# More third-level Strassen steps in a two-layer projection kernel, and some vector work moved to its opening

## The chip, the cores and the metric

The kernel runs on one core of a Trainium2 chip. The metric is the device time of one execution in microseconds; less is better. Everything is fp32.

## The reference, cut to what matters

`x` is 8 x 256 tokens by 1024. Two layers, each with its residual:

```python
# layer 0: one shared weight W, and a rank-16 update per expert, two of eight experts per token
base  = einsum('btd,od->bto', x, W)
gates = softmax of the top 2 of (x @ Wr.T + 5 * one_hot(language_ids)), spread over 8 experts
h     = einsum('btd,erd->bter', x, A)
x     = x + base + 2.0 * einsum('bter,bte,eor->bto', h, gates, B)
# layer 1: every batch row b has its own weight, chosen by an id
x     = x + einsum('bsi,boi->bso', x, weight[adapter_ids])
```

## The kernel before, in words

**The product x W.** It is done by the Strassen-Winograd scheme: with both matrices cut into two by two blocks, seven block products take the place of eight, at the price of sums of blocks. The scheme is used twice. On the first level x, W and the result are cut into halves of 512 (`xb`, `wb`, `yb`, with keys "11" to "22"), and the seven products are called by their keys "1" to "7"; the program does them in the order 1, 2, 5, 6, 3, 7, 4. Product 1 is `opening`, the others are calls of `product`. On the second level, every product is again seven: P1, P2, and so on, on quarters. These pass through three pairs of PSUM banks, called A, X and B. P1 is computed in A, copied to X by ScalarE, and both go on as accumulators; B takes P5 and P3. From one product to the next the roles of the three pairs rotate (`role[:] = [x, b, a]`), so that the next product's A is the pair that was X, and its B the pair that was A.

**The third step.** A second-level product is four matmuls of 512 columns, or, where its number stands in the `leaves` of `make_subs`, seven matmuls of 256 columns: the "leaf" of `third`. Its sums r1 to r4 (128 elements a row) and q1 to q4 (256) are made by VectorE, and its own partial results, P1 and P5, need a bank each, from which `take` evicts them into the result in four parts (of P1, P6, P5 and P7). For leaf 3 these banks are the two of pair X, for the others the two single banks (`singles`), which also serve the gate logits and the transposes of the gates (`turn(1, singles("ps_g_1"))`, after product 2). Before, leaf 2 is taken in all six products after the opening, leaf 3 in product 5, and leaf 4 in products 5, 3 and 4; the opening has leaves 3 and 4 of its own.

**The order of the vector work.** It is set while the program is built, under a manual schedule. `queue` holds vector work that can be done early: the sums of the following products, the first-level sums S1 to S4 of W (`w_sum`), the gates of the second half. A planner keeps two clocks, `now["pe"]` and `now["dve"]`, adds the cost of each instruction by `us(n)`, and puts queued work into VectorE's stream where its clock is behind TensorE's (`ahead`), or at the latest where a matmul needs it (`force`). Evictions are placed by `after` when their matmul is done. VectorE then executes in this order.

**Other work.** `project` makes the gate logits and the low-rank inputs, `gating` the gates. The low-rank update is added inside the products by matmuls with `up[rows]` and `hg`; for the rows "d" they read `bdiff`, the differences of B's rows (`b_differences`). Layer 1 is `adapt`, once per batch row: seven matmul groups in A, X and B with one Strassen-Winograd step, its sums placed by `pump`. Its first unit follows product 4.

Of the kernel before, what the change touches and what calls it, by code (L numbers as in the profile page):

```python
# [25 lines left out]
def kernel(  # L26
# [43 lines left out]
    TQ = TH // 2  # L70
# [219 lines left out]
    def gating(j):  # L290

        m1, hot1, ops1 = first_max(lg[j], j, 1)
        rest = rtile([P, C, E], "rest")
        m2, hot2, ops2 = first_max(rest, j, 2)
        dm = rtile([P, C], "dm")
        ex = rtile([P, C], "ex")
        den = rtile([P, C], "den")
        g1 = rtile([P, C], "g1")
        g2 = rtile([P, C], "g2")
        wide = [P, C, E]  # L300

        def onto_h():
            h = hT[j].rearrange("p c (e r) -> p (c e) r", r=R)
            g = hot1.rearrange("p c e -> p (c e)").unsqueeze(2).to_broadcast([P, C * E, R])
            tt(h, h, g, ALU.mult)


        ops = ops1 + [
            lambda: nc.vector.scalar_tensor_tensor(rest, hot1, NEG, lg[j], ALU.mult, ALU.add)
        ] + ops2 + [  # L310
            lambda: minus(dm, m2, m1),
            lambda: nc.scalar.activation(ex, dm, AF.Exp),
            lambda: nc.vector.tensor_scalar(den, ex, 1.0, None, ALU.add),
            lambda: nc.vector.reciprocal(g1, den),
            lambda: nc.vector.tensor_scalar(g1, g1, SCALING, None, ALU.mult),
            lambda: tt(g2, g1, ex, ALU.mult),
            lambda: tt(hot1, hot1, g1.unsqueeze(2).to_broadcast(wide), ALU.mult),
            lambda: tt(hot2, hot2, g2.unsqueeze(2).to_broadcast(wide), ALU.mult),
            lambda: add(hot1, hot1, hot2),
        ]  # L320
        return [(0.23, f) for f in ops] + [(1.22, onto_h)]

    def turn(j, banks):

# [22 lines left out]
    queue = []  # L347
    done = {}

    def us(n):  # L350
        return (n + 151) / 960

    def vec(t, fn, key=None):
        fn()
        now["dve"] += t
        done[key] = now["dve"]

    def event(name, later=0.0):
        events[name] = now["pe"] + later
# [52 lines left out]
    def third(key, leaf, lhs, rhs, place, what):  # L412

        ra = lambda i, j: lhs()[:, j, ts(i, P)]
        rb = lambda i, j: rhs()[:, i, ts(j, NQ)]
        n0, n1 = slice(0, NQ), slice(NQ, TQ)
        t, own = {}, {}
        at = {"r13": 0, "r2": P, "r4": 2 * P, "q13": 3 * P, "q2": 3 * P + NQ, "q4": 3 * P + 2 * NQ}  # L420
        me = f"{key}:L{leaf}"

        def op(name, tag, fn, x, y, what):
            width = P if name[0] == "r" else NQ

            def run():
                if place == 0:
                    t[name] = sub3.tile([P, width], F32, name=f"{name}_{key}{leaf}", tag=tag)
                else:
                    t[name] = spare(1536 + (place - 1) * 1152 + at[tag], width)  # L430
                fn(t[name], *(t[v] if isinstance(v, str) else v() for v in (x, y)))

            return us(width), what, f"{me}.{name}", run

        A, B = (lambda i, j: lambda: ra(i, j)), (lambda i, j: lambda: rb(i, j))
        ops = [
            op("r1", "r13", add, A(1, 0), A(1, 1), what),
            op("q1", "q13", minus, B(0, 1), B(0, 0), what),
            op("r2", "r2", minus, "r1", A(0, 0), what),
            op("q2", "q2", minus, B(1, 1), "q1", what),  # L440
            op("r4", "r4", minus, A(0, 1), "r2", what),
            op("q4", "q4", minus, B(1, 0), "q2", what),
        ]
        ops3 = [
            op("r3", "r13", minus, A(0, 0), A(1, 0), (f"{me}.5",)),
            op("q3", "q13", minus, B(1, 1), B(0, 1), (f"{me}.5",)),
        ]

        def piece(n, acc=None, banks=None):
            if n in (1, 5):  # L450
                own[n] = (single(f"P{n}_{key}{leaf}", n // 5) if banks is None else banks[n // 5])[:, n0]
            for x in {3: ("r4",), 4: ("q4",), 5: ("r1", "q1"), 6: ("r2", "q2", "P1"), 7: ("r3", "q3", "P6")}.get(n, ()):
                force(f"{me}.{x}")
            out_, l, r = {
                1: lambda: (own[1], ra(0, 0), rb(0, 0)),
                2: lambda: (acc[:, 0, n0], ra(0, 1), rb(1, 0)),
                3: lambda: (acc[:, 0, n1], t["r4"], rb(1, 1)),
                4: lambda: (acc[:, 1, n0], ra(1, 1), t["q4"]),
                5: lambda: (own[5], t["r1"], t["q1"]),
                6: lambda: (own[1], t["r2"], t["q2"]),  # L460
                7: lambda: (own[1], t["r3"], t["q3"]),
            }[n]()
            nc.tensor.matmul(out_, lhsT=l, rhs=r, start=(n in (1, 5)), stop=True, skip_group_check=True)  # L463
            now["pe"] += 0.432
            event(f"{me}.{n}", 0.2)

        def take(n, dest, base=None, sub=False):

            cut = lambda v: {1: v[:, 0, n0], 6: v[:, 0, n1], 5: v[:, :, n1]}[n]
            if n == 7:  # L470
                cut = lambda v: v[:, 1, :].rearrange("p (j n) -> p j n", j=2)
            src = own[5 if n == 5 else 1]
            if n in (5, 7):
                src = src.unsqueeze(1).to_broadcast([P, 2, NQ])
            evict(NQ if n in (1, 6) else TQ, cut(dest), src, None if base is None else cut(base), f"{me}.P{n}", sub)

        return ops, ops3, piece, take

    def make_subs(key, w, x, leaves=(), what=(), last=(), place=0):

# [32 lines left out]
        if 3 in leaves:  # L515
            deep[3] = third(key, 3, lambda: t["s2"], lambda: b(1, 1), 1, (f"{key}:P6",))
        if 4 in leaves:
            deep[4] = third(key, 4, lambda: a(1, 1), lambda: t["t2"], 2, (f"{key}:P6",))
        subs[key] = (a, b, t, late, deep)
        return [  # L520
            op("s1", add, a(1, 0), a(1, 1), what),
# [17 lines left out]
    def multiply(up=None, tokens=None):  # L539


        def mm(acc, lhs, rhs, first=False, rows=None, c=0, part=(0, 1), ms=(0, 1), need=()):
            if rows == "d":
                force("bdiff")
            for key in need:
                force(key)
            steps = [(lhs[:, k, ts(m, P)], rhs[:, k, :], m) for k in part for m in ms] if part else []
            if up is not None and rows is not None:
                steps += [(up[rows][:, ts(m, P)], hg[tokens][:, c, :], m) for m in ms]
            for i, (l, r, m) in enumerate(steps):  # L550
                nc.tensor.matmul(  # L551
                    acc[:, m, :],
                    lhsT=l,
                    rhs=r,
                    start=(first and i < len(ms)),
                    stop=(i >= len(steps) - len(ms)),
                    skip_group_check=True,
                )
                now["pe"] += 0.859

        return mm

    def opening(key, dest):
# [85 lines left out]
        chunk(7)  # L649
        piece(7)  # L650
        out(7, q2)
        out(5, q2, q2)
        add(q2, A, q2)

    def product(key, base, dest, lora=None, tokens=None, sub=False, joined=None):
# [66 lines left out]
        if 3 in deep:  # L722
# [19 lines left out]
            piece(7)  # L742
            take(7, at[1], at[1], sub)
            take(5, at[1], at[1], sub)
        else:
            mm(B, t["s2"], b(1, 1), False, "d", 1, need=K("s4", "B5"))
        put(1, B, True, "B3")
        join(1)
        if 4 in deep:
            if 3 not in deep:  # L750
                piece4(5)
                piece4(6)
                take4(6, at[2], old[2], sub)
                force(f"{key}.A7")
                mm(A, None, None, False, "1", 0, part=())
            for n in (2, 3, 4):
# [228 lines left out]

    opening("1", y21)
    done.clear()
    now["pe"], now["dve"] = 0.0, 3.5
    after(0.4, lambda: take(0, 1))
    for i, (t, f) in enumerate(gating(0)):  # L990
        vec(t, f, "gates0")
    project(1, 0, halves(pair("ps_h_1_0", 2)))
    now["pe"] += 7.5
    subs2 = make_subs("2", "12", "21", (2,))
    run(subs2[:2])
    after(0.4, lambda: take(1, 0))
    run(subs2[2:])
# [11 lines left out]
    event("T2", 30.0)  # L1009
    queue += [(t, (), f"gate{i}", f) for i, (t, f) in enumerate(gating(1))]  # L1010
    gates = queue[-1][2]
    queue += [(0.69, (), "I22", lambda: add_identity(wb["22"]))]
    queue += w_sum(minus, "21", "22", "21", (), "S1")
    queue += [(2.0, (), "bdiff", b_differences)]
    queue += make_subs("5", "21", "12", (2, 3, 4), ("T1",), "2", 1)
    product("2", y21, y11, 0, 0)
    force(gates)
# [3 lines left out]
    add_raw("21", 1, 1)  # L1021
    event("T3", 30.0)
    queue += w_sum(add, "11", "21", "11", (), "S2")
    queue += make_subs("6", "11", "22", (2,), ("T2",), "5", 0)
    product("5", None, y22, 1, 1)
    raw("12", 1, 1)
    event("x22", 14.0)
    queue += w_sum(minus, "12", "11", "12", (), "S4")
    queue += make_subs("3", "12", "12", (2, 4), ("x22",), "6", 1)
    product("6", y21, y21, sub=True)  # L1030
    add_raw("22", 1, 0)
# [3 lines left out]
    product("3", y22, y12, 2, 1, joined=(y12, y21))  # L1035
    load_w1(0, "21", "12", "22", "11")
    event("w0", 18.0)
    queue += make_subs("4", "22", "22", (2, 4), ("T4",), "7", 1)
    product("7", y21, y21, joined=(y22, y21))
    queue += [(t, ("w0",), f"w0_{i}", f) for i, (t, _, f) in enumerate(prep_w1(0, 0))]  # L1040
    y0 = []
# [2 lines left out]
        y0[:] = y0 or prep_y(0)  # L1044
        y0[i][2]()

    queue += [(0.69, ("4:P7", "7:join2"), f"y0_{i}", lambda i=i: prep_y0(i)) for i in range(4)]
    product("4", y21, y21, 1, 0)
    for q in list(queue):
        q[3]()  # L1050
# [57 lines left out]
```

## Time and profile before

| | us |
|---|---|
| median of three runs (lowest, highest) | 425.71 (425.32, 426.33) |
| the profiled execution, its own time | 425.69 |
| its span, first to last instruction | 423.7 |
| TensorE busy | 418.8 |
| VectorE busy | 287.6 |
| ScalarE busy | 40.6 |
| GpSimd busy | 17.6 |
| product 2 starts, with the transposes before it | 58.4 |
| product 5 starts | 90.6 |
| product 6 starts | 120.3 |
| the adapter units start | 227.8 |

How to read it: the profile is of one execution, in us from the first instruction. The lines of vector work all carry one number, L228, that of the helper that issues them; tiles tell them apart (y is a result block, s and t are sums of the second level, r and q of the third; many sums lie in spare room of x11 and show as x). L551 are matmuls of 512 columns, L463 those of the third step, L256 the projections, L326 the transposes of the gates, L863 the adapter units. Matmuls are pipelined: their shown durations overlap, and the step from one start to the next is what each costs in a stream.

### The profile page before, as it was taken

The page shows a single profiled execution, that of the slowest core. Times are in us where ns is not written, and L with a number is a line of the kernel's source. Part 1 is how long each engine was busy: PE and PEld are TensorE (multiplying, and loading weights), DVE is VectorE, ACT ScalarE, POOL GpSimd, SP SyncE. Part 2 cuts the span into 40 slices and gives each one's busy share as a digit, 9 for nine tenths or more (in the row PEclk, how much of TensorE's full clock was granted, in tenths as well). Part 3 has the DMA queues.
Part 4 walks back from the last instruction along what each step waited for, and adds up shares of the span by engine and source line. Part 5 has one row for each costly group of instructions (what it writes and reads, how often), then busy time and mean ns, then how long its engine had stood idle before and what let it go on. Part 6 is the DMA issues. An engine that isn't in the chain of part 4 may idle for free.

```text
span 423.7 us, 3569 instructions
## 1 busy us (share of the span) xinstructions
PE 418.8 (99%) x1294; PEld 226.1 (53%) x1294; DVE 287.6 (68%) x439; ACT 40.6 (10%) x69; POOL 17.6 (4%) x26
## 2 busy tenths in 40 slices
PE   8999999999999999999999999999999999999996
PEld 6579975445655454554555444444444444444574
DVE  1645699957888989878786666765747666665531
ACT  2010120022110000000000101010101101010110
POOL 1000020110001101103000000000000000000000
PEclk9999999999999999999999999999999999999999
DMA  8995089476220964918902384666658385650202
GB/s 274 385 397 236 2 173 210 126 184 101 100 99 4 179 215 78 294 24 155 342 0 99 116 321 159 242 214 213 224 194 300 109 298 190 213 183 0 101 0 99
DMA packets 20257, 72.61 MB, mean 171 GB/s; under 512 B 1552, under 2 KB 3856, under 8 KB 15248
## 3 DMA queue, kind: packets, MB, share of 16 engines
q1 hardware_dynamic: 15088, 58.87, 38.0%
q0 software_dynamic: 3904, 12.58, 16.6%
q10 hardware_dynamic: 1248, 0.93, 0.7%
q8 instruction: 10, 0.16, 0.1%
q14 instruction: 7, 0.06, 0.0%
HBM read 55.61 MB, written 8.39 MB: 151 GB/s over the span
## 4 chain that ended last, share of the span: by engine, by line
PE 99%; POOL 0%; ACT 0%; issue 0%; POOLq 0%
PE A L863 23%; PE A L551 21%; PE B L551 13%; PE B L863 13%; PE ps_h L256 7%; PE X L863 6%; PE P L463 5%; PE A_last L930 3%; PE X L551 3%; PE X L463 2%; PE A L463 1%; PE idle L568 1%; PE B L463 1%; PE ps_g L326 0%; ACT z L960 0%
## 5 line engine op out<-in xcount | busy, mean ns | idle before, releaser
L551 PE MATMUL A<-t,s 128*128 128x512 f32 x112 | 50.3, 592 | 0.0
L863 PE MATMUL B<-x,x 128*128 128x512 f32 x96 | 43.2, 592 | 0.0
L863 PE MATMUL A<-w,x 128*128 128x512 f32 x88 | 39.6, 592 | 0.0
L228 DVE TENSOR_TENSOR w<-w,w 128x1024 f32<-128x1024 f32 x24 | 29.1, 1223 | 15.1 <-PE A L863 15.1
L863 PE MATMUL A<-w,y 128*128 128x512 f32 x88 | 39.1, 592 | 0.0
L256 PEld LDWEIGHTS ps_h<-y,x 128*128 128x128 f32 x256 | 31.7, 190 | 3.3 <-issue 2.9
L551 PEld LDWEIGHTS A<-t,s 128*128 128x128 f32 x112 | 21.2, 190 | 21.2 <-issue 20.6
L256 PE MATMUL ps_h<-y,x 128*128 128x136 f32 x256 | 31.9, 279 | 0.0
L863 PEld LDWEIGHTS B<-x,x 128*128 128x128 f32 x96 | 18.2, 190 | 22.1 <-issue 22.0
L863 PEld LDWEIGHTS A<-w,x 128*128 128x128 f32 x88 | 16.7, 190 | 21.0 <-issue 21.0
L863 PEld LDWEIGHTS A<-w,y 128*128 128x128 f32 x88 | 16.7, 190 | 20.6 <-issue 20.6
L228 DVE TENSOR_TENSOR y<-P,y 128x512 f32<-128x512 f32 (+1 forms) x31 | 17.6, 567 | 14.0 <-PE P L463 9.1
L228 DVE TENSOR_TENSOR y<-A,y 128x1024 f32<-128x1024 f32 x17 | 20.8, 1223 | 8.3 <-issue 4.6
L551 PE MATMUL A<-x,w 128*128 128x512 f32 x56 | 25.4, 594 | 0.0
L551 PE MATMUL B<-x,s 128*128 128x512 f32 x40 | 18.0, 592 | 0.0
L228 DVE TENSOR_TENSOR x<-w,x 128x1024 f32<-128x1024 f32 (+1 forms) x11 | 10.6, 968 | 10.8 <-PE A L863 7.8
L225 ACT ACTIVATE z<-A 128x512 f32<-128x512 f32 x12 | 7.2, 597 | 101.4 <-PE A L863 101.4
L228 DVE TENSOR_TENSOR w<-x,w 128x1024 f32<-128x1024 f32 x8 | 9.7, 1225 | 10.2 <-PE A L863 5.7
L551 PEld LDWEIGHTS A<-x,w 128*128 128x128 f32 x56 | 10.3, 190 | 10.8 <-issue 10.5
L228 DVE TENSOR_TENSOR z<-z,X 128x512 f32<-128x512 f32 x7 | 4.8, 687 | 15.9 <-PE X L863 15.9
L551 PE MATMUL B<-t,s 128*128 128x512 f32 x32 | 15.0, 595 | 0.0
L863 PE MATMUL X<-w,y 128*128 128x512 f32 x32 | 14.4, 592 | 0.0
(179 smaller groups left out, 555.8 us busy)
## 6 DMA issues: line engine op xcount, KB each, us to landing
x<-w_dram SPq DMA_DIRECT2D x24, 1024.0 KB, 5.1
x<-xT_dram SPq DMA_DIRECT2D x10, 1024.0 KB, 10.6
w<-w_dram SPq DMA_DIRECT2D x8, 1024.0 KB, 4.8
out_dram<-z SPq DMA_DIRECT2D x15, 512.0 KB, 3.0
x<-x POOLq DMA_DIRECT2D x4, 1024.0 KB, 9.9
x<-xT_dram POOLq DMA_DIRECT2D x4, 1024.0 KB, 9.3
y<-y POOLq DMA_DIRECT2D x8, 512.0 KB, 5.3
w<-wT_dram SPq DMA_DIRECT2D x3, 1024.0 KB, 15.3
```

The costliest lines, as they stand in the source:

```text
L225: nc.scalar.activation(out_, x, AF.Copy, scale=scale)
L228: nc.vector.tensor_tensor(out_, x, y, op)
L256: nc.tensor.matmul(ps[v][:, u * EA : (u + 1) * EA], lhsT=xk(k, j, c)[:, ts(r, P)], rhs=aw_sb[:, k, :], start=(first and k == some[0] and u ...
L463: nc.tensor.matmul(out_, lhsT=l, rhs=r, start=(n in (1, 5)), stop=True, skip_group_check=True)
L551: nc.tensor.matmul(acc[:, m, :], lhsT=l, rhs=r, start=(first and i < len(ms)), stop=(i >= len(steps) - len(ms)), skip_group_check=True,)
L568: nc.tensor.matmul(idle[:, 0, :P], lhsT=ident, rhs=ident, start=True, stop=True)
L863: nc.tensor.matmul(accs[name], lhsT=lhs[:, k // 2, k % 2, :], rhs=rhs[:, k, :], start=(first and k == 0), stop=(k == KH - 1), skip_group_c ...
L930: nc.tensor.matmul(acc, lhsT=lhs[:, k // 2, k % 2, :], rhs=rhs[:, k, ts(v, m)], start=(first and k == 0), stop=(k == KH - 1), skip_group_c ...
```

## The change

Product 2 takes leaf 4 also (with its sums in a free part of y12), product 6 leaf 4, and product 4 leaf 3. Where leaf 4 is taken without leaf 3, its pieces 5 and 6 now stand between the two halves of B's accumulation, instead of after it. The identity on w22, the sum S1 of W and the differences of B's rows are no longer queued for product 2 but issued in the opening, ahead of the last evictions. S4 is queued before product 5 instead of after it. The planner's constants change: `us(n)` is (n + 66) / 960 instead of (n + 151) / 960, a result counts as ready 0.1 us after its instruction's cost, VectorE's clock starts at 6.0 instead of 3.5, and some listed costs follow.

```diff
@@ gating
-        return [(0.23, f) for f in ops] + [(1.22, onto_h)]
+        return [(0.26, f) for f in ops] + [(us(2 * TQ), onto_h)]
@@ the planner
     def us(n):
-        return (n + 151) / 960
+        return (n + 66) / 960
     def vec(t, fn, key=None):
         fn()
         now["dve"] += t
-        done[key] = now["dve"]
+        done[key] = now["dve"] + 0.1
@@ third
+                elif place == 3:
+                    t[name] = flat(yb["12"])[:, 2048 + at[tag] : 2048 + at[tag] + width]
@@ make_subs
-            deep[4] = third(key, 4, lambda: a(1, 1), lambda: t["t2"], 2, (f"{key}:P6",))
+            deep[4] = third(key, 4, lambda: a(1, 1), lambda: t["t2"], 3 if early else 2, (f"{key}:P6",))
@@ multiply
-            if rows == "d":
-                force("bdiff")
@@ opening
         out(7, q2)
+        add_identity(wb["22"])
+        for f in w_sum(minus, "21", "22", "21"):
+            f[3]()
+        b_differences()
         out(5, q2, q2)
         add(q2, A, q2)
@@ product
+        elif 4 in deep:
+            mm(B, t["s2"], b(1, 1), False, "d", 1, ms=(0,), need=K("s4", "B5"))
+            piece4(5)
+            mm(B, t["s2"], b(1, 1), False, "d", 1, ms=(1,))
+            piece4(6)
+            take4(6, at[2], old[2], sub)
         else:
             mm(B, t["s2"], b(1, 1), False, "d", 1, need=K("s4", "B5"))
...
         if 4 in deep:
             if 3 not in deep:
-                piece4(5)
-                piece4(6)
-                take4(6, at[2], old[2], sub)
                 force(f"{key}.A7")
@@ the order of the products
-    now["pe"], now["dve"] = 0.0, 3.5
+    now["pe"], now["dve"] = 0.0, 6.0
-    subs2 = make_subs("2", "12", "21", (2,))
+    subs2 = make_subs("2", "12", "21", (2, 4), early=True)
-    queue += [(0.69, (), "I22", lambda: add_identity(wb["22"]))]
-    queue += w_sum(minus, "21", "22", "21", (), "S1")
-    queue += [(2.0, (), "bdiff", b_differences)]
...
-    queue += make_subs("6", "11", "22", (2,), ("T2",), "5", 0)
+    queue += make_subs("6", "11", "22", (2, 4), ("T2",), "5", 0)
+    queue += w_sum(minus, "12", "11", "12", (), "S4")
     product("5", None, y22, 1, 1)
     raw("12", 1, 1)
     event("x22", 14.0)
-    queue += w_sum(minus, "12", "11", "12", (), "S4")
...
-    queue += make_subs("4", "22", "22", (2, 4), ("T4",), "7", 1)
+    queue += make_subs("4", "22", "22", (2, 3, 4), ("T4",), "7", 1)
```

More of the change, by code (lines that the diff above doesn't have):

```diff
@@ L477, in third, with make_subs @@
         return ops, ops3, piece, take
-    def make_subs(key, w, x, leaves=(), what=(), last=(), place=0):
+    def make_subs(key, w, x, leaves=(), what=(), last=(), place=0, early=False):
         before = (f"{last}:P7",) if last else ()
@@ L1045, in prep_y0 @@
         y0[i][2]()
-    queue += [(0.69, ("4:P7", "7:join2"), f"y0_{i}", lambda i=i: prep_y0(i)) for i in range(4)]
+    queue += [(0.6, ("4:P7", "7:join2"), f"y0_{i}", lambda i=i: prep_y0(i)) for i in range(4)]
     product("4", y21, y21, 1, 0)
```

## The prediction

> **What bounds the kernel now.** I read the page's busy shares, the chain that ended last, that chain in order of time, and then the timeline where one product hands over to the next.
>
> ```profile
> PE 418.8 (99%) x1294; PEld 226.1 (53%) x1294; DVE 287.6 (68%) x439; ACT 40.6 (10%) x69; POOL 17.6 (4%) x26
> ...
> PE 99%; POOL 0%; ACT 0%; issue 0%; POOLq 0%
> ```
>
> TensorE is the bound and does not pause: 99% of the chain is its own work, and the list of waits names none of TensorE after 38 us. So a matmul removed is worth its whole time, and every new wait of TensorE costs its whole length. VectorE is 68% busy, which says nothing of single moments. Two lines of the chain in order of time price the matmuls:
>
> ```profile
> 118.72 1.29 PE A L463 x6
> ...
> 137.27 3.43 PE B L551 x8
> ```
>
> A matmul of the program is two instructions. At 512 columns (L551) one takes 3.43 / 8 = 0.429 us, at 256 columns (L463) 1.29 / 6 = 0.215 us.
>
> The timeline at the end of product 5 and at the end of product 4, the last one before the adapter stage:
>
> ```profile
> 108.19 0.69 DVE L228 TENSOR_TENSOR y<-P,y 128x512 f32<-128x512 f32 x1 [1.78 <-ACT y L223]
> 108.99 1.23 DVE L228 TENSOR_TENSOR y<-X,y 128x1024 f32<-128x1024 f32 x1
> ...
> 118.76 1.42 DVE L228 TENSOR_TENSOR y<-X,y 128x512 f32<-128x512 f32 x2 [0.97 <-PE X L463]
> ...
> 120.28 3.66 PE L551 MATMUL A<-x,w 128*128 128x512 f32 x8
> ...
> 227.75 3.60 PE L863 MATMUL A<-w,y 128*128 128x512 f32 x8
> 227.95 1.42 DVE L228 TENSOR_TENSOR y<-P,y 128x512 f32<-128x512 f32 x2 [2.22 <-PE P L463]
> 229.40 1.22 DVE L228 TENSOR_TENSOR y<-A,y 128x1024 f32<-128x1024 f32 x1
> ...
> 231.18 3.60 PE L863 MATMUL B<-x,x 128*128 128x512 f32 x8
> ```
>
> At 120.18 VectorE has emptied X of product 5, and at 120.28 product 6 starts writing that bank pair: 0.10 us of cover. At 230.62 it has emptied product 4's A, and the adapter's B, which takes that pair, starts at 231.18: 0.56 us. Such lines also give VectorE's steps from start to start: 1024 elements 1.135 us (108.99 to the next at 110.13), 512 0.60, 256 0.335, 128 0.20, and 0.72 for a 512 whose result the next one needs (two end after 1.42). VectorE starts 0.20 us after a matmul group has made way for the next (227.75 to 227.95).
>
> The opening holds the one wait of TensorE on VectorE:
>
> ```profile
> 36.90 0.69 DVE L228 TENSOR_TENSOR y<-P,y 128x512 f32<-128x512 f32 x1 [3.15 <-PE P L463]
> ...
> 37.65 0.70 PE L463 MATMUL P<-t,w 128*128 128x256 f32 x2
> ```
>
> The bank is free at 37.59, TensorE goes at 37.65, and its pair of instructions takes 0.70 where unhindered pairs take 0.59. So a wait costs its length, 0.06 us of signal, and about 0.10 us to start again.
>
> **What the Trainium skill says.** "VectorE: DVE Perf Modes", section on the TRN2 errata, gives an fp32 add of N elements (N + 151) / 0.96 ns, so 1224 at 1024; the trace has 1223 on average. "Perfetto Trace Analysis", section "Optimizing Scalar/DVE Operations", says that half of an instruction's overhead overlaps the next; the trace agrees (1.135 from start to start against 1.223), and the new cost function in the diff, (n + 66) / 960, gives that 1.135. "PSUM — Partial Sum Buffer", section on bank collisions, says the hardware does not hold a matmul back from a bank that VectorE is reading, so the program must wait; the 37.65 line is such a wait. "TensorE: Matmul & The Clock Gate", section "The mechanism", has matmuls strictly in order, so whatever stands behind a waiting one waits too; nothing in the trace contradicts it.
>
> **The change part by part.**
>
> *Third steps, saved.* Three more: P4 of products 2 and 6, P3 of product 4. Each replaces 8 instructions of 512 columns (3.43 us) by 14 of 256 (14 x 0.215 = 3.00). Saved 0.43, three times 1.29 us, all on the path.
>
> *Third steps, added.* Each gives VectorE four r (0.20) and four q (0.335), 2.14 us, and evictions of 0.335 + 0.335 + 0.72 + 0.72 beside the one of 1024 that was there, 2.11 us. Three steps: 12.8 us more VectorE in 424, mostly in its idle time. Where it is not, the stalls below follow. TensorE's order elsewhere keeps its count: splitting B's second half round pieces 5 and 6 only interleaves.
>
> *S1 and B's differences moved to the opening.* Add to the diagonal, two sums of 1024, four differences: 0.72 + 2.27 + 0.60 + 3 x 0.335 = 4.6 us, put into VectorE's queue at 41.4, where it stood idle from 41.5 to 44.37. The rest of the opening moves 1.6 us later. Cover: w21 is the last weight, issued at 22.3, 17.3 us to landing at most, so there by 39.6; the gates' transpose starts at 58.38 and its last input (ScalarE's copy, 55.72 now) comes at 57.3. The first piece of product 2 at 62.7 needs a bank whose copy then ends at about 62.5: cover of 0.1 to 0.2, taken as nothing, 0 to 0.3 in the range. In product 2 the 4.6 us come free again.
>
> *Stall 1, end of product 2.* P4's third step accumulates in the two single banks, and the very next instructions, the transposes of the second gates (`turn(1, singles(...))`), write these banks. Before, they were long free. Let the last piece end at 0. VectorE takes P7 at 0.20 and P5 at 0.92, done at 0.90 and 1.62. The second four transposes start at 1.68; without the wait they would at 0.43 (8 take 0.87). Stall 1.25, plus 0.10 to start again. Behind it stands all of product 5. The profile before has no such wait; less than 0.4 would need both evictions before the last piece is done, which the data forbid.
>
> *Stall 2, end of product 5.* S4 is queued before product 5 instead of after it, and product 6's early sums come earlier. In the changed program VectorE runs from the line at 108.19 to the X evictions without a gap: 0.80, the two evictions, t2 and r1 in between 3.61, the P1 part 0.335, product 6's leaf sums 1.41, s3 0.60, leaf sums, P6's part and the third sums of product 5 1.41, t3 1.135, S4 2.27: 11.56. The two X evictions end 0.72 + 0.69 later, at 12.97, signal 13.03. TensorE's distance is unchanged, 120.28 - 108.19 = 12.09. Stall 0.94, plus 0.10. Of it S4 alone is 2.27 in the queue; if it slipped behind the evictions, nothing would be left. Range 0.6 to 1.2.
>
> *Stall 3, first adapter unit.* With P3 stepped too, product 4 ends in X (P3's P1, P5), B and A. From the end of P3's piece 7 at 0: evictions start at 0.20 (P7), 0.92 (P5), 1.64 (B, 1.135), 2.78, 3.50 (P4's), 4.21 (A), done at 5.43, signal 5.49. TensorE reaches the adapter's B after four pieces and A, 1.72 + 3.43 = 5.15. Stall 0.34, plus 0.10. Its A needs X at 1.67 and comes at 1.72: just covered. Range 0.2 to 0.6.
>
> *Nothing:* SP's and POOL's queues hold the same transfers in the same order; the half of x12 reloaded after product 5 goes out about 2 us later and has landed at 120.3 and 131.9 for use at 139 and after. The planner's constants and its later start only order the queue. Products 3, 6 and 7 keep 0.2 us or more before every wait by the same sums; up to 0.3 of that might still show.
>
> Sum: 1.35 + 1.04 + 0.44 - 1.29 = +1.54. The profiled execution took 425.69 us (span 423.7, 2.0 around it), the median of three runs 425.71, so the two agree to 0.02. Forecast **427.2 us**, slower by 0.36%.
>
> **The rivals.** A measurement of this kernel can tell about 0.2%, 0.85 us, from no change.
> - *VectorE's idle time takes all of it (faster).* Product 5's stretch has VectorE busy 21.0 of 30.7 us, 6.5 of the idle in one piece before 97.69. If S4 and the added sums fall there, stalls 2 and 3 go, and if the transposes found free banks, stall 1 too: 424.4. Decided at the end of product 2: faster by 0.2% needs all waits together under 0.44. Against it: the banks are the same by name, and stall 1 alone is 1.35.
> - *Only stall 1 is real (no change).* The planner's corrected costs keep VectorE ahead at the two other ends: 425.7 + 1.35 - 1.29 = 425.8, up to 426.5 with part of stall 2. Against it: the order puts S4 ahead of the evictions.
> - *The opening slips too (slower still).* The 1.6 us shift uses up the cover at 62.7 and thin ones later (0.2 each): 428.0. For it: the cover is 0.1 to 0.2. Against: the bank is the first of two copies.
> - *The steps are not made:* excluded, the leaf lists name them.
>
> **How the numbers follow.** Forecast with its slower variant 0.84, no change 0.11, faster 0.05. Low end: stall 1, half of stall 2, none of 3, 426.3; high end: all thin covers gone, 428.1.
>
> **What would show it.** Matmuls of 256 columns up by 42 instructions and of 512 down by 24; waits of TensorE on VectorE at about 90 (transposes, 0.9 and 0.3), 122 (A of product 6, 0.9), 232 (adapter's B, 0.3). If no wait stands at 90, the bank argument is wrong; if the span falls, the rival.

## The result, and the profile after

The changed kernel is slower: 428.27 us (median of nine runs, 427.19 to 428.57) against 425.71 us for the kernel before (nine runs, 425.32 to 426.80). The ratio is 1.0054, with a 95% interval from 1.0044 to 1.0064. The profiled execution of the changed kernel took 428.44 us (span 426.4), that of the kernel before 425.69 (span 423.7). The median lies 0.17 above the high end of the forecast's range (428.1).

From the page after, the busy shares and the chain that ended last:

```profile
PE 419.7 (98%) x1312; PEld 229.8 (54%) x1312; DVE 299.1 (70%) x475; ACT 40.6 (10%) x69; POOL 17.6 (4%) x26
...
PE 92%; DVE 6%; issue 1%; ACT 0%; POOL 0%; POOLq 0%; DVEq 0%
```

VectorE has 11.5 us more work. TensorE is still the bound, but no longer runs through. The 6% of the chain that is now VectorE's is not lost time: nearly all of it is one piece, from 37.8 to 63.8 us, which leads to the pause at 63 below and during which TensorE works too. The records have 42 more matmul instructions of 256 columns and 24 fewer of 512, exactly the three steps. The list of TensorE's waits after (in us: total, times, longest) has three entries that were not there:

```profile
PE idle L568 <- POOL ident masks.py:199: 1.4, 1, 1.4
PE A L551 <- PE P L465: 0.8, 1, 0.8
PE ps_g L326 <- DVE y L228: 0.8, 1, 0.8
PE B L870 <- PE A L870: 0.2, 1, 0.2
```

The first is at the very beginning and is in every kernel here. The others are, in the order of the list, product 6's first matmul, the transposes of the second gates, and the adapter's first B. Two of the three name TensorE itself as the releaser. The timelines below speak against that: in each place an eviction of VectorE ends after the instruction named, just ahead of the start. They show these places one by one (start, duration, then engine, line, operation and tiles; the brackets give idle time and releaser). Modelled matmul ends overlap, so I measure a pause as the step from one start to the next beyond the normal step, and count the slower first instruction after it in.

**At 90, stall 1:**

```profile
90.14 0.60 PE L465 MATMUL P<-y 128*128 128x256 f32 x2
90.77 1.42 DVE L228 TENSOR_TENSOR y<-P,y 128x512 f32<-128x512 f32 x2 [0.36 <-PE P L465]
91.52 1.39 PE L326 MATMUL ps_g<-ident,y 128*128 128x128 f32 x8 [0.78 <-DVE y L228]
```

The last piece of product 2 starts at 90.14, VectorE takes the first of its two banks at 90.77, and the transposes that write these banks begin at 91.52. The eight take 1.39 from first start to last end instead of 1.04, as the second four wait again. Together the places between 90.4 and 92.4 hold 1.30 us more than the normal steps.

**At 122, stall 2:**

```profile
119.60 2.36 DVE L228 TENSOR_TENSOR w<-w,w 128x1024 f32<-128x1024 f32 x2
121.87 1.42 DVE L228 TENSOR_TENSOR y<-X,y 128x512 f32<-128x512 f32 x2
121.97 0.59 PE L465 MATMUL P<-x 128*128 128x256 f32 x2
123.38 2.81 PE L551 MATMUL A<-x,w 128*128 128x512 f32 x6 [0.81 <-PE P L465]
```

S4 (`w<-w,w`, two of 1024) stands directly ahead of the two evictions of X, which end at 123.29. Product 6's first matmul, which takes that pair, follows at 123.38: 0.98 us late, and its first instruction takes 0.07 more, 1.05 in all.

**At 230, stall 3:**

```profile
229.96 1.23 DVE L228 TENSOR_TENSOR y<-B,y 128x1024 f32<-128x1024 f32 x1
230.03 3.67 PE L870 MATMUL A<-w,y 128*128 128x512 f32 x8
231.10 1.41 DVE L228 TENSOR_TENSOR y<-P,y 128x512 f32<-128x512 f32 x2
232.54 1.22 DVE L228 TENSOR_TENSOR y<-A,y 128x1024 f32<-128x1024 f32 x1
233.86 3.67 PE L870 MATMUL B<-x,x 128*128 128x512 f32 x8 [0.17 <-PE A L870]
```

The eviction of A ends at 233.76, the adapter's B starts at 233.86, which costs 0.41 with the slower first instruction. Its A at 230.03 starts in time, but its first instruction takes 0.07 more as well.

**At 63, a place that the prediction had taken as covered:**

```profile
62.06 1.22 DVE L228 TENSOR_TENSOR t<-x 128x1024 f32<-128x1024 f32 x1
63.19 0.25 DVE L228 TENSOR_TENSOR y<-ps_h,bias 128x16 f32<-128x16 f32 x2
63.40 0.65 ACT L273 COPY y<-ps_h 128x256 f32<-128x256 f32 x2 [2.00 <-DVE y L228]
63.82 0.70 PE L465 MATMUL P<-x,w 128*128 128x256 f32 x2
```

The first third-step piece of product 2 needs the bank that ScalarE's copy at 63.40 empties, the copy waits for VectorE's small add at 63.19, and that one stands behind a sum that the opening's move has pushed later. The piece comes 0.26 us late, and its pair of instructions takes 0.105 more: 0.37.

The list of waits shows nothing of this place: it lists only what the profile counts as idle, and a wait of 0.26 us between overlapping matmuls isn't.

**The balance.** Summed, the pauses are 0.37 + 1.30 + 1.05 + 0.41 + 0.07 = 3.20 us; the kernel before had one of 0.07, the slower first instruction of product 6 at 120.28; the three steps save 1.29. That gives +1.84. The timelines of the two kernels measure the same sum. First before, then after: the first weights' matmuls, the small matmul `ids_wide` near the end of the opening's loading phase, and the last group of matmuls of the program.

```profile
4.17 2.59 PE L551 MATMUL X<-x,w 128*128 128x512 f32 x4
...
15.55 0.38 PE L591 MATMUL ids_wide<-ids_f,ones 1*128 1x8 f32 x2
...
416.64 3.62 PE L930 MATMUL A_last<-w,y 128*128 128x256 f32 x16
```

```profile
4.13 3.50 PE L551 MATMUL X<-x,w 128*128 128x512 f32 x4
...
16.42 0.38 PE L591 MATMUL ids_wide<-ids_f,ones 1*128 1x8 f32 x2
...
419.40 3.62 PE L937 MATMUL A_last<-w,y 128*128 128x256 f32 x16
```

From `ids_wide` to it is 401.09 us before and 402.98 after, so **+1.89** is what the change costs, 0.05 more than the sum. The rest of the 2.75 us between the two profiled executions, 0.87, had passed before `ids_wide`: the first four matmuls took 3.50 instead of 2.59. That is no work of the change. The trace's record of the granted clock is at full from 5.43 us before and only from 7.26 after, and instructions ahead of that run at half rate. In the twelve profiles of this study `ids_wide` started anywhere from 15.19 to 16.67, also where the work ahead of it is the same, and its start less half of the time at which the clock came to full is 12.77 to 12.95 in all twelve: the moment of the clock's release sets it. Of its nine runs here, the kernel before had five at 425.3 to 425.7 and four at 426.1 to 426.8. I therefore compare kernels by this **stretch** from `ids_wide` to the last group, beside the timed ratio.

### The profile page after: what moved, and what is told of

It is laid out like the page before. It is cut to its first block, busy times and chain, and to the rows that moved or that the text cites. A ratio compares the mean times of both kernels' runs of the same rounds, so it can differ in the third digit from the quotient of the medians.

```text
span 426.4 us, 3640 instructions
## 1 busy us (share of the span) xinstructions
PE 419.7 (98%) x1312; PEld 229.8 (54%) x1312; DVE 299.1 (70%) x475; ACT 40.6 (10%) x69; POOL 17.6 (4%) x26
## 4 chain that ended last, share of the span: by engine, by line
PE 92%; DVE 6%; issue 1%; ACT 0%; POOL 0%; POOLq 0%; DVEq 0%
PE A L870 23%; PE A L551 19%; PE B L870 13%; PE B L551 12%; PE X L870 6%; PE P L465 5%; PE A_last L937 3%; PE X L551 3%; PE X L465 3%; PE ps_h L256 3%; DVE y L228 2%; PE A L465 2%; PE B L465 1%; DVE t L228 1%; DVE w L228 1%
## 5 line engine op out<-in xcount | busy, mean ns | idle before, releaser
L228 DVE TENSOR_TENSOR y<-P,y 128x512 f32<-128x512 f32 (+1 forms) x35 | 19.8, 565 | 5.9 <-PE P L465 5.6
L551 PE MATMUL B<-x,s 128*128 128x512 f32 x32 | 14.9, 593 | 0.0
L228 DVE TENSOR_TENSOR x<-x 128x1024 f32<-128x1024 f32 (+1 forms) x15 | 14.8, 1006 | 0.0
```

The costliest lines, as they stand in the source:

```text
L228: nc.vector.tensor_tensor(out_, x, y, op)
L551: nc.tensor.matmul(acc[:, m, :], lhsT=l, rhs=r, start=(first and i < len(ms)), stop=(i >= len(steps) - len(ms)), skip_group_check=True,)
```

## The experiments

My theory: the cost is those named pauses, each ended by one eviction or copy, and each can be taken away alone. Rivals: a pause taken away comes back at the next place, since VectorE is simply late; the planner's new constants put everything a little later; the opening's move is the larger loss, and should have stayed undone. The table gives all ten runs; ratios are to the kernel before on the same chip.

| run | us | ratio [95%] | `ids_wide` to last group | against before |
|---|---|---|---|---|
| e1_other_banks | 426.88 | 1.0014 [1.0005, 1.0022] | 417.88 - 16.18 = 401.70 | +0.61 |
| e2_s4_late | 426.98 | 1.0022 [1.0014, 1.0030] | 418.05 - 16.04 = 402.01 | +0.92 |
| e3_opening_undone | 431.86 | 1.0135 [1.0120, 1.0151] | 421.96 - 15.44 = 406.52 | +5.43 |
| e4_steps_only | 432.19 | 1.0148 [1.0132, 1.0164] | 422.13 - 15.19 = 406.94 | +5.85 |
| e5_planner_only | 425.74 | 0.9996 [0.9986, 1.0005] | 417.19 - 16.10 = 401.09 | 0.00 |
| e6_opening_only | 426.61 | 1.0011 [1.0004, 1.0018] | 416.94 - 15.48 = 401.46 | +0.37 |
| e7_three_mended | 425.27 | 0.9982 [0.9972, 0.9991] | 417.00 - 16.67 = 400.33 | -0.76 |
| e8_four_mended | 425.08 | 0.9979 [0.9972, 0.9987] | 416.35 - 16.43 = 399.92 | -1.17 |
| e9_no_p3_of_4 | 427.46 | 1.0031 [1.0019, 1.0043] | 418.50 - 15.56 = 402.94 | +1.85 |
| e10_no_p4_of_6 | 428.31 | 1.0055 [1.0041, 1.0069] | 418.79 - 15.38 = 403.41 | +2.32 |

**Stall 1 alone: other banks for the transposes.** From the changed kernel:

```diff
-    turn(1, singles("ps_g_1"))
+    turn(1, halves(pair("ps_g_1", role[1])))
```

This kernel leaves the right result out: its transposes write in the pair that product 5 takes as its X and accumulates in. The instructions are otherwise the same, so it tells times only.

> The changed kernel with one edit: the second gates are transposed into the pair of banks that the next product calls X (free since B was evicted), not into the two single banks. Theory (banks): the pause of 1.30 us at the transposes goes and nothing takes its place, since the pair is next written by ScalarE's copy 3.4 us later; the kernel before plus 0.5 us (0.53 from 1.83 - 1.30). The pauses at product 6 (1.05) and at the adapter's B (0.4) stay. Rival (VectorE is simply behind): product 5 then waits the same 1.3 us somewhere else, and the time stays about 1.8 us above before.

The timeline at the same place:

```profile
89.91 0.59 PE L465 MATMUL P<-y 128*128 128x256 f32 x2
90.34 1.04 PE L326 MATMUL ps_g<-ident,y 128*128 128x128 f32 x8
91.22 1.02 PE L551 MATMUL A<-x,w 128*128 128x512 f32 x2
```

The transposes follow the piece after 0.43 us, a normal step, and product 5 comes 0.88 later. The stretch fell by 1.28 against the changed kernel (1.30 was the pause), and stalls 2 and 3 kept their size. So this pause does not come back later.

**Stall 2 alone: S4 queued after product 5 again.** From the changed kernel:

```diff
-    queue += w_sum(minus, "12", "11", "12", (), "S4")
     product("5", None, y22, 1, 1)
...
     event("x22", 14.0)
+    queue += w_sum(minus, "12", "11", "12", (), "S4")
```

> The changed kernel with S4 of W queued after product 5 again. Theory: S4's 2.27 us leave the queue ahead of the two evictions of X, so the pause of 1.05 us at product 6's first matmul goes and no new one comes; before plus 0.8 us. Rival (product 6's own earlier sums and the third step make VectorE late, not S4): a pause of 0.5 us or more stays there, or S4 delays product 6 and its pause returns at product 3.

The pause at 122 is gone (its entry is missing from TensorE's waits, the other two stand), and the stretch fell by 0.97 of the 1.05; the rest is the 0.07 of a slower first instruction, which the kernel before has at this place too. S4's two sums lie ahead of the evictions only because of where they are queued.

**The opening's move undone in the changed kernel.** I22, S1 and `bdiff` go back into the queue for product 2, and a matmul that reads `bdiff` forces it again:

```diff
+            if rows == "d":
+                force("bdiff")
...
-        add_identity(wb["22"])
-        for f in w_sum(minus, "21", "22", "21"):
-            f[3]()
-        b_differences()
...
+    queue += [(0.69, (), "I22", lambda: add_identity(wb["22"]))]
+    queue += w_sum(minus, "21", "22", "21", (), "S1")
+    queue += [(2.0, (), "bdiff", b_differences)]
```

> The changed kernel with the identity on w22, S1 and B's differences back in the queue for product 2. Theory: the pause of 0.37 us at 63 goes, but product 2 has VectorE busy 27.9 of 30.7 us in the kernel before, and P4's third step adds 4.25 us; with S1 and the differences there as well (4.6 us, in the 27.9) VectorE is 1.5 us or more over the stretch, so new pauses of 2 to 4 us in all stand in product 2 or at its end: before plus 3.5 to 5.5 us. Rival (the move costs and gains nothing else): before plus 1.5 us.

The timeline in the middle of product 2, and below it the window 82 to 88 (length; busy time and count of PE, PEld, DVE, ACT, POOL; granted clock; DMA share; GB/s):

```profile
81.39 1.22 DVE L228 TENSOR_TENSOR w<-w,w 128x1024 f32<-128x1024 f32 x1
82.52 1.36 DVE L228 TENSOR_TENSOR bdiff<-b_sb 128x512 f32<-128x512 f32 x3
83.60 2.02 PE L553 MATMUL B<-hg,bdiff 128*128 128x512 f32 x2 [1.95 <-DVE bdiff L228]
85.41 1.06 PE L465 MATMUL P<-y 128*128 128x256 f32 x2
86.26 2.30 PE L553 MATMUL B<-x,s 128*128 128x512 f32 x4
```

```profile
82.00:88.00 6.00, 4.40 (x8) 2.20 (x9) 6.00 (x11) 0.00 (x0) 0.36 (x1) 0.72 0.89 139
```

VectorE is busy for all 6.00 us of the window. S1 and then `bdiff` come directly before the matmul that reads `bdiff`, and TensorE pauses 2.11 us. Then something new: the two matmul instructions from 83.60 take 1.81 us (normal 0.86), the two of 256 columns from 85.41 take 0.85 (normal 0.43), the four from 86.26 take 2.14 (normal 1.72). That is 1.79 us more, with a granted clock of 0.72 over the window; the trace has the clock at half from 83.68 to 87.10, for 3.41 us. The pause at 63 is gone (-0.37), stalls 1 to 3 are as in the changed kernel: 2.11 + 1.79 - 0.37 = 3.53, and the stretch rose by 3.54. The move thus saves 3.9 us within this change and costs 0.37.

**The three steps alone, in the kernel before,** without the move, S4's place or the constants (P4's sums in product 2 have their place in y12 as in the change):

```diff
-    subs2 = make_subs("2", "12", "21", (2,))
+    subs2 = make_subs("2", "12", "21", (2, 4), early=True)
...
-    queue += make_subs("6", "11", "22", (2,), ("T2",), "5", 0)
+    queue += make_subs("6", "11", "22", (2, 4), ("T2",), "5", 0)
...
-    queue += make_subs("4", "22", "22", (2, 4), ("T4",), "7", 1)
+    queue += make_subs("4", "22", "22", (2, 3, 4), ("T4",), "7", 1)
```

> The kernel before with the three third steps alone: nothing moved, the planner's constants as before, P4's pieces 5 and 6 behind B. Theory: the matmuls save 1.29 us, but product 2 is over its VectorE time as in the run without the opening's move, and the transposes and the adapter's B still wait: before plus 2 to 5 us. S4 is not early, so no pause at product 6's first matmul. Rival (the steps gain, the moves and constants lose): before minus 0.5 to 1.3 us.

The timeline at the end of product 2, and the window 92 to 96 (columns as above):

```profile
90.19 0.70 PE L465 MATMUL P<-y 128*128 128x256 f32 x2 [1.36 <-DVE y L228]
91.19 1.22 DVE L228 TENSOR_TENSOR t<-x 128x1024 f32<-128x1024 f32 x1
92.33 1.41 DVE L228 TENSOR_TENSOR y<-P,y 128x512 f32<-128x512 f32 x2
93.07 1.85 PE L326 MATMUL ps_g<-ident,y 128*128 128x128 f32 x8 [2.18 <-DVE y L228]
94.71 3.71 PE L553 MATMUL A<-x,w 128*128 128x512 f32 x6
```

```profile
92.00:96.00 4.00, 2.93 (x10) 2.19 (x11) 2.93 (x4) 1.19 (x2) 1.28 (x1) 0.65 0.15 20
```

A pause of 1.53 ahead of the last piece, one of 2.34 ahead of the transposes, and again a slow phase after the long one, worth about 1.7 us (the clock at half from 93.24 to 96.65). There is no pause at 122, since S4 is in its old place; stall 3 is there, and pauses between 148 and 156, at the end of product 6 and in the first part of product 3, come to 0.77 us more. The result, +5.85, is above the 2 to 5 that I expected: I had counted pauses and no slow phase.

**The constants alone, and the opening's move alone,** each in the kernel before. The constants are those of the diff in `us`, `vec` and `gating`, with VectorE's clock at 4.4; the move is the reverse of e3's edit, with the clock at 6.0.

> The kernel before with the planner's constants alone (its later start of VectorE's clock set to 4.4, since nothing is added to the opening). Theory: the constants only reorder VectorE's queue, which has room; TensorE keeps its order and waits nowhere: before, within 0.3 us. Rival (part of the loss is the new order itself): a pause at a hand-over, before plus 0.5 to 1 us.

> The kernel before with S1, the identity and B's differences moved to the opening, and nothing else but the planner's later start. Theory: the later copies of the gate logits make TensorE pause at the first piece of product 2, 0.37 us with the restart, as in the changed kernel, and the 4.6 us that VectorE gains in product 2 buy nothing without P4's third step there: before plus 0.3 to 0.4 us. Rival (the pause at 63 belongs to P4's third step): no pause, no difference.

The constants move the stretch by 0.00. The move alone costs +0.37, and the timeline has it as one pause at 62.9, 0.26 us and 0.105 for a slower start: the very pause of the changed kernel, so it belongs to the move and not to the steps. VectorE's timeline shows where its cover went. The last eviction of the opening and the sum with A behind it, before and then with the move alone:

```profile
44.37 0.69 DVE L228 TENSOR_TENSOR y<-P,y 128x512 f32<-128x512 f32 x1 [2.90 <-ACT y L223]
45.17 1.23 DVE L228 TENSOR_TENSOR y<-A,y 128x1024 f32<-128x1024 f32 x1
```

```profile
45.92 0.68 DVE L228 TENSOR_TENSOR y<-P,y 128x512 f32<-128x512 f32 x1
47.12 1.22 DVE L228 TENSOR_TENSOR y<-A,y 128x1024 f32<-128x1024 f32 x1 [0.52 <-DVE y L228]
```

The eviction comes 1.55 us later, but the sum 1.95, since it follows after 1.20 instead of 0.80; what stands behind it moves by 1.95 too, down to the small add ahead of the copy, 62.27 against 60.32 (this profile's `ids_wide` is 0.06 earlier, so 1.61 and 2.01 of shift). Why the sum waits 0.4 longer the trace does not tell.

**The mends together.** If the pauses are independent, a kernel with the steps and without the pauses must gain. From the changed kernel: the transposes of the second gates go into the middle of product 2, where the single banks are free; S4 is queued late; `bdiff` alone is queued again, S1 stays in the opening (VectorE's clock 4.4).

```diff
-        mm(A, t["s3"], t["t3"], need=K("s3", "t3", "A6"))
+        mm(A, t["s3"], t["t3"], part=(0,), need=K("s3", "t3", "A6"))
+        mid()      # product 2 alone: force(gates), turn(1, singles("ps_g_1"))
+        mm(A, t["s3"], t["t3"], part=(1,))
```

> The changed kernel with three pauses taken away: the second gates are transposed inside product 2, between the halves of its P7, when the single banks have long been emptied; S4 is queued after product 5 again; B's differences go back to product 2's queue, S1 stays in the opening. Theory (the pauses are the whole loss and add up): 1.30 + 1.05 + 0.37 less than the changed kernel, whose matmuls and pauses come to 1.83 above before: 0.9 below before. The pause at the adapter's B (0.4) stays. Rival (VectorE's total is the limit, a pause taken away comes back later): within 0.4 of before or above it, with new pauses in products 5 to 7.

The timeline in the middle of product 2:

```profile
77.13 1.88 PE L553 MATMUL A<-t,s 128*128 128x512 f32 x4
77.33 1.42 DVE L228 TENSOR_TENSOR y<-P,y 128x512 f32<-128x512 f32 x2 [0.32 <-PE P L465]
78.85 1.04 PE L326 MATMUL ps_g<-ident,y 128*128 128x128 f32 x8
```

The four A matmul instructions from 77.13 give VectorE the 1.42 us to empty both banks (done at 78.75), and the transposes start at 78.85 without a pause. Only stall 3 (0.41) and the two slower first instructions, 0.07 each, at product 6's and the adapter's A were left. The stretch is 0.76 below the kernel before, which has one of the two: -1.29 + 0.41 + 0.07 gives -0.81, so 0.05 stays open, as in the changed kernel.

The fourth mend: product 4 alone evicts B after A instead of ahead of it, since the adapter's B takes A's pair first.

```diff
-        put(1, B, True, "B3")
+        if key != "4":
+            put(1, B, True, "B3")
...
             put(2, A, True, "A4")
+            if key == "4":
+                put(1, B, True, "B3")
```

> As the three mended, and the last product evicts B after A, so that the 1.135 us of that eviction stand behind the one that the adapter's B waits for. Theory: the pause at the adapter's B goes (0.33 and 0.08 to restart), 0.07 of a wait on transfers stays: 1.3 below before, the whole saving of the three third steps. Rival: B's eviction, now last, delays the adapter's third group, which writes that bank, or its sums, and the pause comes back within the first unit.

The timeline at product 4's end, then the chain that ended last from this kernel's page:

```profile
227.39 3.67 PE L879 MATMUL A<-w,y 128*128 128x512 f32 x8
227.59 1.42 DVE L228 TENSOR_TENSOR y<-P,y 128x512 f32<-128x512 f32 x2 [0.31 <-PE P L465]
229.04 1.22 DVE L228 TENSOR_TENSOR y<-A,y 128x1024 f32<-128x1024 f32 x1
230.18 1.21 DVE L228 TENSOR_TENSOR y<-B,y 128x1024 f32<-128x1024 f32 x1
230.89 2.31 PE L879 MATMUL B<-x,x 128*128 128x512 f32 x5
```

```profile
PE 99%; POOL 0%; ACT 0%; issue 0%; POOLq 0%
```

A is empty at 230.26, and the adapter's B starts at 230.89, 3.50 after its A: no pause of 0.41 any more. TensorE has the chain at 99% again. With 0.9979 [0.9972, 0.9987] it is faster than both given kernels. Its ratio can't be told from e7's, but its stretch is 0.41 shorter, the size of stall 3. Against the kernel before it has 1.17 us of the 1.29 that the steps were worth; 0.07 of the rest is the slower first instruction of the adapter's A, which is no wait on transfers, as I had taken it: e9 below, without P3's step in product 4, doesn't have it.

**One step taken away, where it has a pause and where it has none.**

```diff
-    queue += make_subs("4", "22", "22", (2, 3, 4), ("T4",), "7", 1)     # e9
+    queue += make_subs("4", "22", "22", (2, 4), ("T4",), "7", 1)
...
-    queue += make_subs("6", "11", "22", (2, 4), ("T2",), "5", 0)        # e10
+    queue += make_subs("6", "11", "22", (2,), ("T2",), "5", 0)
```

> The changed kernel without P3's third step in product 4. Theory: the matmuls take 0.43 us more and the pause at the adapter's B (0.33 and 0.08 to restart) goes, since X's two evictions and their 1.4 us no longer stand ahead of A's: the changed kernel within 0.1 us, so this step bought nothing there. Rival (that pause comes from P4's third step or the new order): it stays, and the time is 0.4 above the changed kernel.

> The changed kernel without P4's third step in product 6. Theory: no pause of the changed kernel stands at product 6's end or in product 3, so nothing but the matmuls changes: 0.43 us more, 2.3 above before. Rival (the step's 4.25 us of VectorE feed the later pauses): the pause at the adapter's B shrinks and the time stays or falls.

Without P3 of product 4 the stretch is 0.04 shorter than that of the changed kernel: 0.43 us of matmuls came back, the pauses at 230 and 233 (0.48) went. The step bought nothing in the changed kernel. Without P4 of product 6 it is 0.43 longer, and no pause changed: that step is worth just its matmuls. It also shows that stall 2 is not this step's doing.

## Why the prediction was right, step by step

The direction and the places held, and each stall's size to 0.1 us: forecast +1.54, measured +1.89 in the stretch. The medians differ by more, +2.56 (see below).

- *Third steps, saved* (1.29): e10 alone measures one of them, 0.43. The 0.05 that stays open in the changed kernel and in e7 may lie here; no run measures the three together.
- *Stall 1* (1.25 + 0.10): 1.30 in the trace, 1.28 when taken away in e1. The argument by the names of the banks was right.
- *Stall 2* (0.94 + 0.10): 1.05, and e2 gave back 0.97 of it by the place of S4 alone. The working came out too: VectorE runs from the eviction at 110.31 to those of X at 121.87 for the 11.56 us of the sum. The "0.10 us of cover" at 120.28 was no full cover: the first instruction there takes 0.07 more already before.
- *Stall 3* (0.34 + 0.10): 0.41, and e8 took it away by the order of two evictions. The adapter's A, "just covered" by 0.05, started in time, with the same 0.07 on its first instruction.
- *S1 and B's differences moved*, "taken as nothing, 0 to 0.3 in the range": **this term was mis-sized.** It cost 0.37 (e6), 0.26 of waiting and 0.105 to start again. The chain of bank, copy and small add had been found. What failed is the shift of the opening, put at 1.6 us: that is right for the last eviction (1.61), but from the sum with A on it is 2.0, and the 0.4 more are above the cover of 0.1 to 0.2 that 1.6 would have left. The price of the cover being gone was not in the sum, and the start-up after a pause was left out of the bound. The half of the rival "the opening slips too" was real, its other half, thin covers elsewhere, was not.
- That in product 2 the moved work "comes free again" was said without a number. e3 gives it: 3.9 us, with the slow phase.
- *Nothing for the constants and queues*: e5 has 0.00.

The rival that VectorE's idle time takes all, and the one that only stall 1 is real, both fall by the traces: all three stalls stand where they were put, and e1, e2 and e8 take each away separately (e8 on top of e7), without its coming back. Between the stretch, +1.89, and the medians, +2.56, lies 0.67. The moment at which the clock came to full, worth 0.87 between the two profiled executions, is enough to explain it, and the forecast had no term for it; that it does in the timed runs, which have no trace, was not shown.

## What to carry to other kernels

Where one engine runs without a gap, a step that saves it work pays its whole saving only if every bank or tile it uses is free again when the next user comes: work out, at each hand-over, who writes the bank next and what stands ahead of its eviction in the other engine's queue. Such waits are mended by order (an eviction of the bank needed first, a sum behind the evictions) or by moving the next user into the middle of the product, and not by less work. In this kernel a cover of 0.1 to 0.2 us was gone once something ahead of it moved, with 0.1 us to start again, and hand-overs covered by 0.05 and 0.10 us still cost 0.07.

## What was not expected of the hardware

- After TensorE had paused for 2.11 us (e3) and for 2.34 (e4), its instructions ran at half rate, 0.85 us instead of 0.43 for 512 columns. The trace has the clock at half for 3.41 us in both, beginning 0.1 and 0.2 us after TensorE had resumed, which added 1.79 and about 1.7 us. In e4 the pause of 1.53 stands only 0.54 us of work ahead of the long one, so e3 is the plainer case. The pauses of about 1 us in the changed kernel (0.95 and 0.23 at stall 1, 0.98 at stall 2) left the clock at full and cost 0.05 to 0.1 to start again, that of 1.53 in e4 0.1. The Trainium skill, "TensorE: Matmul & The Clock Gate", section "What's actually happening", gives half the clock after an idle window of some 3.4 us; the rate agrees, the length does not: in e3 a single pause of 2.11 us was enough. Two cases don't tell where the limit is.
- The same section calls that window free-running and the number of slow first matmuls variable. That fits the first matmuls here (3.50 against 2.59 us for the same four), and the clock's coming to full between 4.49 and 7.52 us over twelve profiles. In a kernel whose changes are worth 1 us this is the largest part of the scatter between the profiles, and a stretch that begins after it is the better measure.
